# Layer 0 of a two-layer graph network: seven products for eight in its maps, edges counted by pairs of columns, and a residual added by a DMA

## The chip, the cores and the metric

The kernel runs on one core of one Trainium2 chip. The metric is the device time of one execution in microseconds (us), lower is better. The core has five engines that run side by side and meet at semaphores: PE (matrix products), DVE (vector), ACT (scalar functions), POOL (GpSimd) and SP (which only issues DMAs). ACT and POOL issue DMAs too, and all DMAs share 16 DMA engines.

## The reference

The input is x, 4096 rows of 512, and adj, a 4096 × 4096 matrix of 0 and 1 with about 32 ones a row. Two graph layers follow one another.

```
# layer 0
keep   = (adj > 0) and (cumsum of it along the row <= 64)    # the first 64 neighbours
cnt    = number kept in the row
xj     = leaky_relu((keep @ x) / max(cnt, 1) @ W_nb.T + b_nb)
xi     = leaky_relu(x @ W_line.T + b_line)
x1     = layernorm(x + xi + (xj where cnt > 0, else 0))
# layer 1
Wh     = x1 @ W + b_W
e_ij   = leaky_relu_0.2(Wh_i . a1 + b1 + Wh_j . a2 + b2), minus infinity where adj is 0
out    = layernorm(x1 + softmax_j(e) @ Wh)
```

## The kernel before

All rows are in 32 blocks of 128. Instruction order is written out by hand; each engine takes its instructions strictly in that order, and only semaphores hold it. The program has three stages.

**Maps of layer 0** (the loop over i in 0..31). Since keep @ x @ W_nb.T is keep @ (x @ W_nb.T), the kernel maps x first. For each block, POOL loads x in a turned form into one of three buffers (`load_turned_x`, tile c), DVE finishes the transposition (`turn_x`, tile xt), and PE computes two products, `linear(xt, "nb")` and `linear(xt, "line")` (L345). Each is four f32 matmuls with 512 columns over the four quarters of the contraction; the trace has two records for each f32 matmul. The first product y is kept on the chip as two terms, y_hi (rounded, ACT, L413) and y_lo (the rest, DVE, L435), so that the sums can use a fast format. The second gets its bias on DVE (`line`, L375), leaky_relu on ACT (`bend`, L379), x added on DVE (`own`, L383; x comes in a second, plain load to tile xb), and is written to memory (own_d).

Beside the maps, the adjacency is turned into codes, in 64 steps (32 blocks by two halves of 2048 columns). A step loads 1 MB of int32 (SP, L160), makes 0/1 edges in bf16 (ACT, `edge`, L167), scans along the row a counter that falls by one at each edge and stops at a floor of 2 (DVE, `scan`, L179), multiplies edges by the counter (L184), packs the result to a byte (ACT, `pack`, L202) and stores it (POOL, code_d). A byte of 2 or more means a kept edge, 1 an edge that is beyond the 64th, 0 none. AHEAD = 20 of these steps are placed in the maps. `fold_w` (L361) folds W with a1 and a2, once, in block 0; its result goes to memory (wa_d).

**Sums of layer 0** (the loop over s, 32 rows of blocks × 4 groups). For row block i, a DMA with transposition brings the codes of its 128 rows (ktb, issued on SP two rows ahead, L460), ACT turns 8 blocks of it at a time into 0/1 weights (`make_kt`, L254), and PE adds 64 matmuls for the row (y_hi and y_lo by turns, L521). The remaining code steps are spread over these rows at RATE / 4 a group (`codes_step`; ACT's share of a step waits in a queue and is taken out one part at a time by `codes_late`). A row is finished one row later in five parts on DVE (`finish`): scaled by 1/cnt with bias (L479), leaky_relu (ACT, L472), added to own, which SP has loaded from own_d (L516 and L485), normalized with a power on POOL (rs, L126), written as x1 (POOL, L492), and multiplied with the folded weights (L497).

**Layer 1** follows and is not touched (L825 and L739 are its products).

Of the kernel before, what the change touches and what calls it, by code (L numbers as in the profile page):

```python
# [9 lines left out]
F32 = mybir.dt.float32  # L10
# [10 lines left out]
P = 128  # L21
# [11 lines left out]
def two_layer_adj_gnn(  # L33
# [43 lines left out]
    two, steep, far, neg_half = few[:, 0:1], few[:, 1:3], few[:, 3:4], few[:, 4:5]  # L77
    for k, value in enumerate((2.0, -0.5 * STEEP, -1.5 * STEEP, FAR, -0.5)):
        nc.vector.memset(few[:, k : k + 1], value)
# [57 lines left out]
    with ExitStack() as l0:  # L137
        adj_p = l0.enter_context(tc.tile_pool(name="l0_adj", bufs=2))
        big = l0.enter_context(tc.tile_pool(name="l0_big", bufs=1))
        y_hi = big.tile([P, NB, C], F32R, name="y_hi")  # L140
        y_lo = big.tile([P, NB, C], F32R, name="y_lo")
# [20 lines left out]

        def edge(s):
            if s < NB * NCH:
                b, h = divmod(s, NCH)
                edge_of[s] = adj_p.tile([P, CH], BF16, name="edge")
                nc.scalar.activation(  # L167
                    edge_of[s], loaded.pop(s), AF.Sigmoid, bias=steep[:, 0:1], scale=STEEP,
                    accum_out=cnts[:, h, b : b + 1],
                )  # L170

        def scan(s):
            if s < NB * NCH:
                b, h = divmod(s, NCH)

                left = adj_p.tile([P, CH], BF16, name="left")
                e = edge_of.pop(s)
                end = ends[:, b : b + 1]
                nc.vector.tensor_tensor_scan(  # L179
                    left, two.to_broadcast([P, CH]), e,  # L180
                    NEIGHBORS + 2.0 if h == 0 else end, ALU.max, ALU.subtract,
                )
                nc.vector.tensor_copy(end, left[:, CH - 1 : CH])
                nc.vector.tensor_tensor(left, e, left, ALU.mult)  # L184
                seen_of[s] = left
# [3 lines left out]
        def count(b):  # L189
            two_b = slice(b, b + 2)  # L190
            cnt = stat.tile([P, 2], F32, name="cnt")
            nc.vector.tensor_scalar(cnt, ends[:, two_b], 2.0, -1.0, ALU.max, ALU.mult)
            nc.vector.tensor_scalar_add(cnt, cnt, NEIGHBORS + 2.0)
# [4 lines left out]
        def pack(s):  # L198
            if 0 <= s < NB * NCH:
                b, h = divmod(s, NCH)  # L200
                code = adj_p.tile([P, CH // 2], BF16, name="code")
                nc.scalar.copy(code.bitcast(U8), seen_of.pop(s))  # L202
# [57 lines left out]
        with ExitStack() as la:  # L260
# [3 lines left out]
            AHEAD = 20  # L264
# [15 lines left out]
            def load_own_x(i, queue):  # L280
                xbs[i] = work.tile([P, C], F32, name="xb", bufs=3)
                queue.dma_start(xbs[i], x_blk(i))

            def turn_by_pe(dst, src):

                t = work.tile([P, C], F32, name="t")
# [6 lines left out]
            def turn_x(i):  # L293
                if i < NB:
                    xts[i] = work.tile([P, NC, P], F32, name="xt", bufs=3)
# [46 lines left out]
            def linear(lhs_t, name):  # L342
                pl = ps_acc.tile([P, C], F32, name="acc")
# [13 lines left out]
            def fold_w():  # L357
                for c in range(NC + 1):
                    wn = raw["w"][c] if c < NC else early_rows[2]
                    for k in range(2):  # L360
                        nc.vector.scalar_tensor_tensor(  # L361
                            early_rows[3], wn, 1.0, early_rows[k], ALU.mult, ALU.mult,
                            accum_out=wa[:, k, c : c + 1] if c < NC else ca[:, k : k + 1],
                        )
# [8 lines left out]
            def line(i):  # L373
                lines[i] = work.tile([P, C], F32, name="t")
# [6 lines left out]
            def own(i):  # L381
                y = xbs.pop(i)
                nc.vector.tensor_tensor(y, y, lines.pop(i), ALU.add)  # L383
                nc.gpsimd.dma_start(own_d[i], y)

# [9 lines left out]
            spin(12)  # L395
            turn_x(0)
            turn_w("nb", 2)
            for i in range(NB):
                if i > 1:
                    load_own_x(i - 1, nc.gpsimd)  # L400
                if i > 0:
                    load_turned_x(i + 4)
                    turn_x(i + 2)
                xt = xts.pop(i)
                pys[i] = linear(xt, "nb")
                if i == 0:
                    turn_w("line")
                pls[i] = linear(xt, "line")
# [540 lines left out]
```

## Time and profile before

| What | Value |
|---|---|
| Median of 3 runs | 1600.48 us (1599.47 to 1602.02) |
| Profiled execution | 1600.12 us, of which the span from first to last instruction is 1598.4 us |
| Maps, from the first product to the first sum | 9.6 to about 235 us |
| Sums | about 236 to 700 us |
| Layer 1 | 700 us to the end |
| Busy of the span: PE, DVE, ACT, POOL | 99%, 82%, 58%, 16% |
| Granted PE clock | 0.997 of full |

A line of a group of instructions gives the kernel's line, engine, operation, written and read tile, shape and number, then the busy time, the mean of one in ns, and idle time before it with what ended that. The chain of waits follows the end of the program back through what released each instruction; a piece gives its start, its length and its work. In a timeline a row gives start, length, engine, line, operation and the number merged, and in brackets how long the engine had been idle and what released it.

### The profile page before, as it was taken

To read this page: it belongs to the slowest core of one execution; us is meant where nothing else is said; L and a number is where in the kernel's file an instruction comes from. 1 tells how busy PE (TensorE), PEld (TensorE's weight loads), DVE (VectorE), ACT (ScalarE), POOL (GpSimd) and SP (SyncE) were. 2 spreads that over 40 slices of the span, in tenths; PEclk is the share of its full clock that TensorE was granted. 3 is DMA by queue.
4 is the path that set the end of the run, shared out by engine and by line. 5 is a ranking of instruction groups with operands and counts; after the bars stand their busy time and mean duration, and the time that the engine had idled before them with its cause. 6 is when DMAs were issued, how large, how long until landed. Compare 5 with 4: busy or idle time off the path is not lost.

```text
span 1598.4 us, 18483 instructions
## 1 busy us (share of the span) xinstructions
PE 1579.6 (99%) x6456; PEld 1218.4 (76%) x6456; DVE 1305.4 (82%) x2154; ACT 924.2 (58%) x1086; POOL 260.0 (16%) x396
## 2 busy tenths in 40 slices
PE   8999999999999999999999999999999999999997
PEld 4444448888888888864378888888888888888886
DVE  4999986999999999555888887878888888788863
ACT  2655556777777777514237755557755557655520
POOL 4455531122223122210000000000000000000000
PEclk9999999999999999999999999999999999999999
DMA  8887867676757666444201111111111111211100
GB/s 195 287 259 236 265 217 224 215 220 211 229 189 228 206 215 191 116 103 122 76 27 28 53 54 41 52 36 34 53 47 47 48 28 44 54 41 53 40 7 33
DMA packets 168364, 192.73 MB, mean 121 GB/s; under 512 B 101408, under 2 KB 134464, under 8 KB 160080
## 3 DMA queue, kind: packets, MB, share of 16 engines
q1 hardware_dynamic: 147968, 131.38, 29.4%
q0 software_dynamic: 19728, 59.27, 11.0%
q8 instruction: 50, 0.82, 0.2%
q10 hardware_dynamic: 576, 0.92, 0.2%
q14 instruction: 42, 0.34, 0.1%
HBM read 132.65 MB, written 42.08 MB: 109 GB/s over the span
## 4 chain that ended last, share of the span: by engine, by line
PE 92%; DVE 3%; DMA 2%; issue 1%; ACT 1%; SPq 0%; POOL 0%; DVEq 0%; POOLq 0%; ACTq 0%
PE acc L739 34%; PE acc L521 29%; PE pt L739 14%; PE acc L345 9%; PE acc L825 5%; DMA c<-in_x_dram 1%; DVE left L179 1%; DMA a<-in_L_gnn_W_line_dram 1%; DMA edge<-in_L_gnn_a_dram 0%; DVE edge L361 0%; DVE xt L299 0%; DMA w<-x_d 0%; DVE y_lo L435 0%; DVE t L375 0%; ACT w L635 0%
## 5 line engine op out<-in xcount | busy, mean ns | idle before, releaser
L521 PE MATMUL acc<-y_hi,kt 128*128 128x512 f32 x1016 | 395.2, 389 | 0.0
L521 PE MATMUL acc<-y_lo,kt 128*128 128x512 f32 x1016 | 395.2, 389 | 0.0
L739 PE MATMUL acc<-bt,s 128*128 128x256 f32 x1536 | 342.6, 379 | 0.0
L739 PEld LDWEIGHTS acc<-bt,s 128*128 128x128 f32 x1536 | 291.8, 190 | 39.7
L635 ACT ACTIVATE w<-nat,few 128x1024 f32<-128x1024 uint8 x128 | 136.9, 1135 | 290.1 <-DVE a L699 238.8
L126 POOL TENSOR_TENSOR rs<-ve,few 128x1 f32<-128x1 f32 x64 | 76.2, 1191 | 969.3 <-DVE ve L124 969.2
L739 PE MATMUL acc<-bt,a 128*128 128x256 f32 x1024 | 232.1, 379 | 0.0
L739 PE MATMUL pt<-bt,a 128*128 128x256 f32 x1024 | 231.5, 379 | 0.0
L521 PEld LDWEIGHTS acc<-y_hi,kt 128*128 128x128 f32 x1016 | 190.8, 188 | 39.7
L521 PEld LDWEIGHTS acc<-y_lo,kt 128*128 128x128 f32 x1016 | 190.6, 188 | 39.5
L739 PEld LDWEIGHTS pt<-bt,a 128*128 128x128 f32 x1024 | 194.6, 190 | 26.9 <-issue 0.5
L254 ACT ACTIVATE kt<-ktb,few 128x1024 fp32r<-128x1024 uint8 x124 | 142.9, 1152 | 124.7 <-PE acc L521 107.8
L739 PEld LDWEIGHTS acc<-bt,a 128*128 128x128 f32 x1024 | 194.6, 190 | 26.5
L699 DVE STREAM_TRANSPOSE a<-w 128x1024 f32<-128x1024 f32 x128 | 153.0, 1224 | 57.8 <-ACT w L680 53.2
L627 ACT ACTIVATE w<-w,st_n 128x1024 f32<-128x1024 f32 x128 | 149.4, 1233 | 39.5 <-DVE m L638 39.5
L638 DVE CUSTOM_DVE_ANT_0 w<-e_n,w 128x1024 f32<-128x1024 f32 x128 | 149.6, 1221 | 9.6 <-ACT w L635 8.2
L167 ACT ACTIVATE edge<-a,few 128x2048 bf16<-128x2048 int32 x64 | 127.4, 1991 | 43.4 <-DVE left L184 20.3
L680 ACT ACTIVATE w<-w,nm 128x1024 f32<-128x1024 f32 x128 | 145.4, 1136 | 11.3 <-DVE nm L671 11.3
L179 DVE TENSOR_TENSOR_SCAN left<-few,edge 128x2048 bf16<-128x2048 f32 x32 | 141.3, 4415 | 12.7 <-ACT edge L167 10.9
L179 DVE TENSOR_TENSOR_SCAN left<-few,ends,edge 128x2048 bf16<-128x2048 f32 x32 | 143.2, 4475 | 2.3 <-ACT code L202 2.3
L202 ACT CAST code<-left 128x2048 uint8<-128x2048 bf16 x64 | 120.5, 1882 | 0.0
L345 PE MATMUL acc<-wt_nb,xt 128*128 128x512 f32 x256 | 115.5, 594 | 2.8 <-DVE xt L299 2.0
(135 smaller groups left out, 1521.3 us busy)
## 6 DMA issues: line engine op xcount, KB each, us to landing
a<-in_adj_dram SPq DMA_DIRECT2D x64, 1024.0 KB, 5.3
code_d<-code POOLq DMA_DIRECT2D x64, 256.0 KB, 3.7
nat<-code_d SPq DMA_DIRECT2D x256, 64.0 KB, 2.0
own_d<-xb POOLq DMA_DIRECT2D x32, 256.0 KB, 5.9
w<-x_d SPq DMA_DIRECT2D x128, 64.0 KB, 2.0
c<-in_x_dram POOLq DMA_DIRECT2D x124, 64.0 KB, 5.6
xb<-in_x_dram POOLq DMA_DIRECT2D x31, 256.0 KB, 5.8
own<-own_d SPq DMA_DIRECT2D x31, 256.0 KB, 2.8
```

The source lines that it names most:

```text
L167: nc.scalar.activation(edge_of[s], loaded.pop(s), AF.Sigmoid, bias=steep[:, 0:1], scale=STEEP, accum_out=cnts[:, h, b : b + 1],)
L179: nc.vector.tensor_tensor_scan(left, two.to_broadcast([P, CH]), e, NEIGHBORS + 2.0 if h == 0 else end, ALU.max, ALU.subtract,)
L202: nc.scalar.copy(code.bitcast(U8), seen_of.pop(s))
L254: nc.scalar.activation(kts[s], bytes_.rearrange("p t (i r) -> p t r i", r=2), AF.Sigmoid, bias=steep[:, 1:2], scale=STEEP,)
L345: nc.tensor.matmul(pl, lhs_t[:, k, :], w_t[name][:, k, :], start=(k == 0), stop=(k == NC - 1),)
L521: nc.tensor.matmul(accs[i], kt[:, k // 2, k % 2, :], term[:, j, :], start=(j == 0 and term is y_hi), stop=(j == NB - 1 and term is y_lo),)
L627: nc.scalar.activation(dst, src, AF.Prelu, bias=bias, scale=scale, alpha=0.2)
L635: nc.scalar.activation(w_i, nats[b, i // 2].bitcast(U8)[:, i % 2, :], AF.Relu, bias=far, scale=-FAR)
L638: nc.vector.tensor_tensor_reduce(w_i, e2_n, w_i, 1.0, -3e38, ALU.subtract, ALU.max, m4s[b][:, i : i + 1])
L680: nc.scalar.activation(w_i, w_i, AF.Exp, bias=nms[b][:, i : i + 1], accum_out=z4s[g][:, r, i : i + 1])
L699: nc.vector.transpose(a[:, r].rearrange("p s (i a) -> p i s a", a=SQ), wts[2 * g + r][:, :, ts(k, 8 * SQ)].rearrange("p i (s x) -> p i s x ...
L739: nc.tensor.matmul(banks[g][n], lhs[:, j, :], bt[:, 4 * k + j, rhs, :], start=(k == 0 and j == 0 and n == mate[0]), stop=(k == NP - 1 and ...
```

## The change

**Seven products.** Blocks 2 to 25 are taken in 12 pairs. A pair's x is a 2 × 2 matrix of quarters (two blocks of rows by two halves of the contraction), and the two weights are another (two halves of the contraction by nb and line). Their product takes seven products of quarters where it took eight, by Winograd's form; each is two matmuls. Sums of the weights (t1, t2, t4, and t3 in the place of w12) are made once, sums of x (s1, s2, s4, and a21 in place) for each pair, all on DVE. The products add in PSUM: bank_y, bank_z, bank_w and three banks taken in turn for x_g. Between products, ACT copies a bank to another or to SBUF and puts the line's bias into bank_z, and DVE adds a line's part into bank_w. A pair's last products stand in the next pair's step, where its line's bend, own and y terms are too. Blocks 0 and 1 and the last six keep the old form; the y terms of the last six lie in the room that the sums had.

**Pairs of columns.** `edge` writes even columns to the first half of the tile and odd columns to the second (it reads int32 at a step of two). `scan_sums` adds both halves and scans 1024 sums with a floor of 3; `scan_codes` adds the odd edge back for the even column's counter and multiplies. `pack` writes its bytes at a step of two. The threshold that tells a kept edge moves from 1.5 to 2.5.

**x by a DMA.** `own` no longer adds x (but for block 31), and the second load of x in the maps goes. In the sums SP loads x itself into the own tile, and one group later POOL issues a DMA that reads own_d and adds it to the tile.

**Order.** `fold_w` is cut in parts that stand in pair 1. AHEAD is 14 and RATE 57/32. In each pair from the second on, one code step stands in four places between the products.

```diff
-    for k, value in enumerate((2.0, -0.5 * STEEP, -1.5 * STEEP, FAR, -0.5)):
+    for k, value in enumerate((3.0, -0.5 * STEEP, -2.5 * STEEP, FAR, -0.5)):
...
+        ONE_BY_ONE = 6
+        EDGE = NB - ONE_BY_ONE
...
         def edge(s):
...
-                    edge_of[s], loaded.pop(s), AF.Sigmoid, bias=steep[:, 0:1], scale=STEEP,
+                    edge_of[s], loaded.pop(s).rearrange("p (t q) -> p q t", q=2),
+                    AF.Sigmoid, bias=steep[:, 0:1], scale=STEEP,
...
+        def scan_sums(s):
...
+                nc.vector.tensor_tensor(left[:, 0], e[:, 0], e[:, 1], ALU.add)
                 nc.vector.tensor_tensor_scan(
-                    left, two.to_broadcast([P, CH]), e,
-                    NEIGHBORS + 2.0 if h == 0 else end, ALU.max, ALU.subtract,
+                    left[:, 1], three.to_broadcast([P, CH // 2]), left[:, 0],
+                    NEIGHBORS + 3.0 if h == 0 else end, ALU.max, ALU.subtract,
                 )
...
+        def scan_codes(s):
...
+                nc.vector.tensor_tensor(left[:, 0], left[:, 1], e[:, 1], ALU.add)
                 nc.vector.tensor_tensor(left, e, left, ALU.mult)
...
-                nc.scalar.copy(code.bitcast(U8), seen_of.pop(s))
+                nc.scalar.copy(
+                    code.bitcast(U8).rearrange("p (t q) -> p q t", q=2), seen_of.pop(s)
+                )
...
-            AHEAD = 20
+            AHEAD = 14
...
             def own(i):
-                y = xbs.pop(i)
-                nc.vector.tensor_tensor(y, y, lines.pop(i), ALU.add)
+                y = lines.pop(i)
+                if i == NB - 1:
+                    nc.vector.tensor_tensor(y, y, xbs.pop(i), ALU.add)
                 nc.gpsimd.dma_start(own_d[i], y)
...
+            def turn_pair(g, r):
+                i = 2 * g + r
+                turn_x(i, (top, low)[r](g) if i < EDGE else None)
+                load_turned_x(i + 3)
...
+            def sums_x(g):
+                a11, a21, a22 = top(g)[:, 0:2], low(g)[:, 0:2], low(g)[:, 2:4]
+                tt(s1, a21, a22, ALU.add)
+                tt(a21, a11, a21, ALU.subtract)
+                tt(s2, s1, a11, ALU.subtract)
...
+            def sum4_x(g):
+                tt(s4, top(g)[:, 2:4], s2, ALU.subtract)
...
+            def product(bank, lhs, rhs, start=False):
+                for k in range(2):
+                    nc.tensor.matmul(
+                        bank, lhs[:, k, :], rhs[:, k, :], start=start and k == 0, stop=k == 1,
...
+            tt(t1, w12, w11, ALU.subtract)
+            tt(t2, w22, t1, ALU.subtract)
...
+            tt(t4, w21, t2, ALU.subtract)
+            tt(w12, w22, w12, ALU.subtract)
+            t3 = w12
...
+            def seven(g, last, codes):
...
+                p = g - 1
...
+                if new:
+                    product(x_g, top(g)[:, 0:2], w11, start=True)
+                if old:
+                    y_low = y_terms(2 * p, bank_y)
+                    y_low()
+                if new:
+                    turn_pair(g + 1, 0)
+                    nc.scalar.copy(bank_y, x_g)
+                if old:
+                    product(x_p, low(p)[:, 0:2], t3)
+                codes[0]()
+                if new:
+                    turn_pair(g + 1, 1)
+                    product(bank_z, s1, t1)
+                if old:
+                    tt(tp, tp, x_p, ALU.add)
+                if new:
+                    nc.scalar.copy(tg, bank_z)
+                    nc.scalar.copy(bank_z, bias_line)
+                if old:
+                    nc.scalar.activation(tp, tp, AF.Prelu, alpha=SLOPE)
+                    product(bank_w, s4, w22)
+                codes[1]()
+                if old:
+                    nc.scalar.activation(t0, bank_w, AF.Prelu, alpha=SLOPE)
+                    own_pair(2 * p + 1, tp)
+                if new:
+                    sum4_x(g)
+                    product(x_g, s2, t2)
+                codes[2]()
+                if old:
+                    own_pair(2 * p, t0)
+                if new:
+                    tt(bank_w, tg, x_g, ALU.add)
+                if old:
+                    product(x_p, low(p)[:, 2:4], t4)
+                if new and 2 * g + 2 < EDGE:
+                    sums_x(g + 1)
+                codes[3]()
+                if old:
+                    y_terms(2 * p + 1, x_p)()
+                if new:
+                    product(bank_y, top(g)[:, 2:4], w21)
...
+            for g in range(1, EDGE // 2):
...
+                if g == 1:
+                    steps = [
+                        lambda: (load_adj(1), fold_w(0)),
+                        lambda: (fold_w(1), fold_w(2)),
+                        idle[0],
+                        lambda: (fold_w(3), fold_w(NC), fold_end(), edge(0)),
+                    ]
+                elif g > 1:
+                    steps = [
+                        lambda: (load_adj(q + 2), edge(q + 1)),
+                        lambda: scan_sums(q),
+                        lambda: pack(q - 1),
+                        lambda: scan_codes(q),
+                    ]
+                    done[0] += 1
+                seven(g, False, steps)
...
+                codes_until(AHEAD if i >= EDGE + 2 else AHEAD - 2 + i - EDGE)
...
-        RATE = 25 / 16
+        RATE = 57 / 32
...
-                    nc.sync.dma_start(owns[i], own_d[i])
+                    nc.sync.dma_start(owns[i], x_blk(i))
+            if g == 3 and i < NB - 1:
+                nc.gpsimd.dma_start(owns[i], own_d[i], accum_op=ALU.add)
```

## The prediction

> **What bounds the kernel now.** I read the page's busy line first, then the chain of waits in order of time, then a table of windows, then the timelines of the early maps, because the change rewrites that stage.
>
> ```profile
> PE 1579.6 (99%) x6456; PEld 1218.4 (76%) x6456; DVE 1305.4 (82%) x2154; ACT 924.2 (58%) x1086; POOL 260.0 (16%) x396
> ...
> 84.44 151.33 PE acc L345 x352
> 235.78 464.03 PE acc L521 x2047
> ...
> 100.00:140.00 40.00, 40.00 (x95) 17.76 (x94) 39.52 (x44) 21.54 (x24) 21.95 (x40) 1.00 0.77 252
> 300.00:400.00 100.00, 100.00 (x443) 82.79 (x442) 93.42 (x116) 75.89 (x68) 22.38 (x25) 1.00 0.70 213
> ```
>
> PE is the bound, and the chain confirms what a busy share alone would not: from 84 us to 236 it is nothing but the maps' products (L345), then 464 us of sums (L521). The windows (after the length: PE, PEld, DVE, ACT, POOL busy, clock, DMA share, GB/s) add the runner-up: VectorE is at 99% beside the maps and at 93% beside the sums. Every us of PE that goes is worth a us only while DVE has less to do than PE.
>
> ```profile
> 43.83 3.60 PE L345 MATMUL acc<-wt_line,xt 128*128 128x512 f32 x8
> 48.37 3.70 PE L345 MATMUL acc<-wt_nb,xt 128*128 128x512 f32 x8 [0.94 <-DVE xt L299]
> 51.91 3.60 PE L345 MATMUL acc<-wt_line,xt 128*128 128x512 f32 x8
> 56.60 3.70 PE L345 MATMUL acc<-wt_nb,xt 128*128 128x512 f32 x8 [1.10 <-DVE xt L299]
> ...
> 47.01 0.68 DVE L435 TENSOR_TENSOR y_lo<-acc,y_hi 128x512 fp32r<-128x512 f32 x1
> 47.61 0.70 DVE L299 STREAM_TRANSPOSE xt<-c 128x512 f32<-128x512 f32 x1
> 48.24 0.65 DVE L375 TENSOR_TENSOR t<-acc,bias_line 128x512 f32<-128x512 f32 x1
> 48.81 0.67 DVE L383 TENSOR_TENSOR xb<-xb,t 128x512 f32<-128x512 f32 x1
> 49.41 4.47 DVE L179 TENSOR_TENSOR_SCAN left<-few,ends,edge 128x2048 bf16<-128x2048 f32 x1
> ...
> 349.10 4.60 POOL L126 TENSOR_TENSOR rs<-ve,few 128x1 f32<-128x1 f32 x1
> ...
> own<-own_d SPq DMA_DIRECT2D x31, 256.0 KB, 2.8
> x_d<-own POOLq DMA_DIRECT2D x31, 256.0 KB, 2.4
> ```
>
> Start to start, a map (8 records, 4 matmuls) takes 3.43 us, and PE stopped twice, 0.94 and 1.10 us, for a transpose stuck behind a scan. DVE instructions start 0.58 to 0.62 us apart; I use these spacings for its load.
>
> **What the Trainium skill says.** (1) "VectorE: DVE Perf Modes", The perf-mode tier table: a bf16 tensor_tensor of 2048 takes 1224 ns, two elements a cycle, f32 one. The trace agrees: L184 1225 ns, f32 L375 of 512 654 ns. My estimate from that page's count (N/2+151 cycles at 0.96 GHz) for the new 1024-wide bf16 add is 0.69 us. (2) "SBUF — State Buffer", the note on cachelines under the DMA port swizzle: lines are 16 bytes and two hits in each suffice. An int32 step of 8 bytes has two. The trace shows only the kin: kt reads uint8 at a step of two bytes, 1152 ns. (3) Same page, Who interferes with whom: a DVE instruction with two SBUF inputs holds up a GpSimd instruction that reads SBUF. The trace shows it: rs takes 0.56 us, but 4.60 beside the scan above. (4) "Collectives: The Full Stack", The bandwidth ceiling: an add in the DMA needs two source reads. No accumulating DMA is in this trace.
>
> **The change, part by part.**
>
> *Products.* Blocks 0 and 1 and 26 to 31 keep 8 matmuls each; 12 pairs take 7 products of 2 matmuls, 14 for 16. So 24 matmuls, 48 records, go. The chain gives 151.33/352 = 0.430 us a record: **−20.6 us** on the bound. A pair now takes 14 × 0.86 = 12.0 us of PE, formerly 13.8, if the operands are early.
>
> *DVE beside the maps, per pair.* Before: 4 instructions a block, 2 × (0.60 + 0.63 + 0.57 + 0.60) = 4.8 us, and 1.4 code steps of 5.84 (4.45 + 0.15 + 1.23), together 13.1 of 13.8. After: y_lo and transpose twice, 2.5; two 512-wide adds on PSUM, nearest row L375, 1.2 (the one that writes PSUM is new: 0.58 to 0.75 each); four 256-wide adds at 0.425 (L612), 1.7; a code step. That step scans half as many, (4.42 − 0.15)/2 + 0.15 = 2.3, plus 0.15, two new adds at 0.69 and L184's 1.23: 5.05. With counts (0.2) **10.7 of 12.0**. DVE gains room instead of losing it.
>
> *Order on PE.* With the pair starting at 0, I put the queues against each other. ACT copies y_hi at 0.1, DVE's y_lo ends 1.4, two transposes 2.7, the add on tp waits for t3's product and ends 4.2, the scan 7.3, s4 7.7; the add into bank_w waits for s2·t2 (8.6) and ends 9.3; s1, a21, s2 of the next pair 10.5, codes 12.3, y_lo 12.9. PE wants bank_w settled at 13.8, s1 at 15.5, bank_y's copy (2.4) at 6.9, tp's at 8.6. All are 4 us or more early. ACT has y_hi 2 × 0.57, three copies 1.7, two Prelu 1.25, edge 2.2, code 1.9: 8.2 of 12.0. POOL loses one xb issue a block and issues 11 × 0.56 = 6.2. Zero on the path; DVE's 1.3 us spare is the cover. Were it gone, PE would wait for s1 first, but with 4 us in hand.
>
> *Front of the stage.* t1, t2, t4 and t3 are four 1024-wide f32 adds (estimate 1.22 each by page (1)'s count), and fold_w (L361, ten of 0.74) moves from 18.7 us into pair 1. I follow both queues from the trace. PE ends the maps of block 1 at 26.7 as before. DVE then does line(1) to 27.4, t4 and t3 to 29.8, two transposes and the first six folds to 35.5, s4 to 35.9, bank_w to 36.6, s1 to s2 37.8, the last four folds 40.8, y_lo of block 2 41.4. ACT's bias reaches bank_z at 28.7, where PE wants it at 28.4: 0.35 lost. Pair 1 has four products (pair 0 has none to finish), so PE wants bank_w at 35.6: 1.0 lost. ACT can refill bank_y at 42.1, wanted at 41.8: 0.35 lost. Together +1.7. The two waits shown above (2.0) should go, as the x loads start earlier and have no xb between them. The wa_d write moves with the fold: issued at 24.5 us it landed 11.2 us later; now it goes out at 41, in front of edge 2 and x block 9. A wait of 5 us on ACT or DVE there is about what PE has in hand: +1.0, bounds 0 and +5. Sum for the front **+0.7**, from −2 to +5.
>
> *Sums stage.* Its products are the same 2048, 464 us. AHEAD falls from 20 to 14 and RATE rises from 50/32 to 57/32, so codes end in row 28 both times. Per row of 14.5 us: DVE 13.55 (93.4%) + 57/32 × 5.05 − 50/32 × 5.84 = 13.4; ACT 11.0 + 7/32 × 4.06 = 11.9; both below 14.5. rs is held by a scan half as long. The extra 7/32 step (1.25 MB) adds about 0.9 us to the DMAs' 10.2 a row. The first code is due far later than it is made; the margin near row 29 is one to two steps, as before. Zero.
>
> *x by DMA.* In the maps 31 DVE adds and 31 POOL loads go (counted above). In the sums SP loads x where it loaded own_d: zero. The accumulating DMA is new, on POOL, after SP's load: 31 issues. POOL is idle most of the time. Its landing: at best x_d's 2.4 to own's 2.8 us, at worst two reads at the busy maps' 5.9 (own_d's landing there), 11.8. I take 5. In the trace it would go out after rs at 353.7, and L485 wants it at 364.0: 9 to 10 us. Behind it on POOL stand x_d of the row before and codes, and for those SP's next own and ktb. With 5 us all is hidden: 0; engine share +0.7 to +2 us of a row, giving 12 to 13.1 of 14.5.
>
> *The rest.* Constants 3 and −2.5, count, and the restored w12 (1.2 us on DVE under nb of block 26) cost nothing: PE has 3.4 us of product beside the last.
>
> *Sum.* The profiled execution took 1600.12 (span 1598.4 and 1.7 around); −20.6 + 0.7 = 1580.2. The median of the runs is 0.36 higher: **1580.5**.
>
> **The rivals.**
>
> *A. Part is lost again.* The wa_d burst, late x blocks, or DMA bursts in the sums (share 70% before, up to 90% after) outrun PE's 4 us. For it: DMA share 1.02 in 40 to 50 us, landings to 14.4 us. Against: PE lost just 2 us there with DVE at 99%. Two or three waits of 3 to 5 us: 1585 to 1597, say 1590.
>
> *B. The accumulating DMA stops DVE: slower.* L703 waits for it once a row, and behind it stand the scans. The cycle rs → accumulate → own → stats → rs takes 3.6 us and the landing L; it fits 14.5 us up to L = 10.7. Each us beyond costs a us in each of 31 rows, after some 15 us of code margin. It passes the gain of 20 at L = 10.7 + 35/31 = 11.8, just my upper bound. At 13 us: 1580 + 71 − 15 = 1636. Against it: 256 KB transfers land in 2.4 to 2.8 us here.
>
> *C. The pairs of columns are dear.* If stepped int32 reads run at half rate, an edge gains 1.7 us, ACT goes to 14.9 a row, and 0.4 × 29 rows give 1592; if the stepped byte writes do too, 1680. If the bf16 adds ran at one a cycle, DVE would go to 15.3: 1603. Against: pages (1) and (2), and kt.
>
> *D. The products aren't shortened.* If waits at each of 84 products cost 0.2 us, 17 us return: about 1597. The present maps have the same kind of waits and start 3.43 us apart without a gap.
>
> **How the numbers follow.** Full gain, 1577 to 1585: 0.66. A: 0.17. D or a mixture ending near 1600: 0.03. B: 0.08. C: 0.06, two thirds of it slower or level. A measurement can tell some 0.2% (3.2 us) from no change: faster 0.84, same 0.04, slower 0.12. The range takes the full case and A: 1576 to 1597.
>
> **What would show it.** Chain: the maps in one piece to about 216 us where they ended at 236, then the sums, still 464 us without a gap. Rows: 12-us pairs; DVE in the maps below 92%; the scan of 1024 near 2.3 us, adds near 0.69; edge still 2.0, code 1.9. The accumulate should land in 3 to 8 us, and DVE's own should not wait for it. Wrong if PE waits more than 5 us in all for DVE or ACT during the maps, or at all in the sums.

## The result, and the profile after

The changed kernel takes **1581.8 us** (1579.91 to 1582.52) where the kernel before, beside it, took 1601.0: ratio 0.9879, 95% interval 0.9862 to 0.9896. Its profiled execution took 1579.91 us, with a span of 1578.1.

The page's busy line, and then the chain of waits in order of time (start, length, work; the long pieces):

```profile
PE 1558.7 (99%) x6408; PEld 1209.3 (77%) x6408; DVE 1257.6 (80%) x2304; ACT 953.7 (60%) x1123; POOL 240.6 (15%) x397
```

```profile
44.49 130.71 PE acc L489 x300
183.79 34.33 PE acc L371 x80
218.12 464.24 PE acc L741 x2048
682.36 41.21 PE acc L1045 x96
```

PE has 48 records fewer and DVE 48 us less, and the sums are still one piece of 464.2 us. But the maps' piece begins only at 44.49: PE stopped just ahead of it. For all that follows I use two marks in the trace, the first product of the maps (its start varies from 9.3 to 12.0 us between executions, with the loads of the weights) and the first sum. **Maps**, between the two: 225.59 us before (9.62 to 235.21), 207.65 after (9.91 to 217.56), so 17.94 less. **Sums**, from the first sum to layer 1: 465.39 before, 464.80 after.

The table of windows (after the length: PE, PEld, DVE, ACT, POOL busy, granted clock, DMA share, GB/s):

```profile
40.00:60.00 20.00, 17.38 (x37) 7.34 (x36) 13.54 (x23) 13.12 (x19) 7.00 (x13) 0.91 0.74 134
...
80.00:120.00 40.00, 40.00 (x94) 17.67 (x93) 34.16 (x54) 27.58 (x37) 21.57 (x40) 1.00 0.63 204
...
300.00:400.00 100.00, 100.00 (x443) 82.77 (x442) 91.59 (x147) 82.85 (x71) 24.46 (x34) 1.00 0.86 257
```

Beside the steady pairs DVE is at 85% where it was at 99%, and beside the sums at 92%; PE is full in both. The one bad window is the first: PE lacks 2.6 us and its clock is low. PE's timeline there:

```profile
32.58 3.60 PE L489 MATMUL acc<-wt_nb,xt 128*128 128x512 f32 x8
36.45 1.98 PE L489 MATMUL acc<-wt_line,xt 128*128 128x512 f32 x4 [0.28 <-DVE acc L574]
38.27 1.88 PE L489 MATMUL acc<-hi,lo 128*128 128x512 f32 x4
39.99 1.88 PE L489 MATMUL acc<-wt_line,lo 128*128 128x512 f32 x4
44.49 2.54 PE L489 MATMUL acc<-hi,lo 128*128 128x512 f32 x4 [2.62 <-ACT acc L548]
46.82 3.07 PE L489 MATMUL acc<-hi,xt 128*128 128x512 f32 x4
49.73 3.60 PE L489 MATMUL acc<-wt_nb,xt 128*128 128x512 f32 x8
```

Groups of four records start 1.72 us apart as a rule, and 1.82 where the first of them follows a stop. Behind the stop of 2.62 us (for L548, ACT's refill of bank_y) the next two groups take 2.33 and 2.91 from start to start: in this execution the stop is followed by a low clock that costs another 1.7 us. The queue of ACT tells why the refill came late:

```profile
40.37 2.13 ACT L175 ACTIVATE edge<-a,few 128x2048 bf16<-128x2048 int32 x1 [6.80 <-DVE edge L386]
42.41 0.19 ACT L175 ACTIVATION_READ_ACCUMULATOR edge<-a,few 128x1 f32 x1
42.50 0.56 ACT L417 CAST y_hi<-acc 128x512 fp32r<-128x512 f32 x1
43.87 0.57 ACT L548 COPY acc<-acc 128x512 f32<-128x512 f32 x1 [0.81 <-DVE y_lo L418]
```

The first edge step stands in front of y_hi on ACT and waits for DVE's fold (L386; the fold's tiles are the edge tiles), though the product that y_hi reads (the first half of PE's row at 32.58; the other half is the next pair's first product) had ended at about 34.5. y_lo waits for y_hi, the refill for y_lo, PE for the refill.

The groups (busy us, mean ns, then idle before and its cause) and the DMA rows (KB, median us to landing) of the new operations:

```profile
L175 ACT ACTIVATE edge<-a,few 128x2048 bf16<-128x2048 int32 x64 | 136.2, 2129 | 11.8 <-DVE edge L386 6.8 <-issue 2.7 <-DVE left L206 1.5
...
L194 DVE TENSOR_TENSOR_SCAN left<-few,ends,left 128x1024 bf16<-128x1024 f32 x32 | 75.2, 2351 | 1.1
...
L193 DVE TENSOR_TENSOR left<-edge 128x1024 bf16<-128x1024 bf16 x64 | 43.6, 682 | 9.7 <-ACT code L223 9.7
...
L736 POOL DMA_DIRECT2D own<-own_d x31 | 28.7, 925 | 17.2 <-DMA own<-in_x_dram 16.3 <-issue 0.8
```

```profile
own<-own_d POOLq DMA_DIRECT2D x31, 256.0 KB, 5.1
x_d<-own POOLq DMA_DIRECT2D x31, 256.0 KB, 4.7
```

The scan takes half, the new adds 0.68 us, and the accumulating DMA lands in 5.1 us. The edge step costs 0.14 us more than before (1991 ns), where the prediction had expected it unchanged.

### The profile page after: what moved, and what is told of

The parts are those of the page before. It is cut to its first block, busy times and chain, and to the rows that moved or that the text cites. A ratio compares the mean times of both kernels' runs of the same rounds, so it can differ in the third digit from the quotient of the medians.

```text
span 1578.1 us, 18600 instructions
## 1 busy us (share of the span) xinstructions
PE 1558.7 (99%) x6408; PEld 1209.3 (77%) x6408; DVE 1257.6 (80%) x2304; ACT 953.7 (60%) x1123; POOL 240.6 (15%) x397
## 4 chain that ended last, share of the span: by engine, by line
PE 95%; DMA 2%; DVE 2%; ACT 1%; issue 1%; SPq 0%; POOL 0%; POOLq 0%; DVEq 0%; ACTq 0%
PE acc L959 35%; PE acc L741 29%; PE pt L959 14%; PE acc L489 8%; PE acc L1045 5%; PE acc L371 2%; DMA a<-in_L_gnn_W_line_dram 1%; DMA c<-in_x_dram 1%; PE pt L371 0%; DMA w<-x_d 0%; DVE edge L386 0%; ACT w L855 0%; DMA own_d<-t 0%; DVE c L809 0%; POOL c L298 0%
## 5 line engine op out<-in xcount | busy, mean ns | idle before, releaser
L741 PE MATMUL acc<-y_hi,kt 128*128 128x512 f32 x824 | 320.5, 389 | 0.0
L741 PE MATMUL acc<-y_lo,kt 128*128 128x512 f32 x824 | 320.5, 389 | 0.0
L126 POOL TENSOR_TENSOR rs<-ve,few 128x1 f32<-128x1 f32 x64 | 46.7, 730 | 945.8 <-DVE ve L124 933.1
L741 PEld LDWEIGHTS acc<-y_hi,kt 128*128 128x128 f32 x824 | 154.7, 188 | 32.2
L741 PEld LDWEIGHTS acc<-y_lo,kt 128*128 128x128 f32 x824 | 154.6, 188 | 32.1
L175 ACT ACTIVATE edge<-a,few 128x2048 bf16<-128x2048 int32 x64 | 136.2, 2129 | 11.8 <-DVE edge L386 6.8
L1045 PE MATMUL acc<-w,c 128*128 128x512 f32 x232 | 100.3, 593 | 2.6 <-DVE c L809 2.6
L1045 PEld LDWEIGHTS acc<-w,c 128*128 128x128 f32 x232 | 43.9, 190 | 58.8 <-issue 52.1
L206 DVE TENSOR_TENSOR left<-edge,left 128x2048 bf16<-128x2048 bf16 x64 | 78.4, 1225 | 2.2
```

Source lines behind the costliest of these rows:

```text
L175: nc.scalar.activation(edge_of[s], loaded.pop(s).rearrange("p (t q) -> p q t", q=2), AF.Sigmoid, bias=steep[:, 0:1], scale=STEEP, accum_ou ...
L741: nc.tensor.matmul(accs[i], kt[:, k // 2, k % 2, :], term[j], start=(j == 0 and term is y_hi), stop=(j == NB - 1 and term is y_lo),)
L1045: nc.tensor.matmul(pws[s], x1t[:, m, :], ws[:, m, :], start=(m == 0), stop=(m == NC - 1))
```

## The experiments

The theory: the 24 matmuls that go are the whole gain; the other two parts bring little by themselves, but make the room on DVE without which the seven products could not be kept fed; what is missing in the maps is one order on ACT. The rivals are in each expectation. Each ratio is to the kernel before on the same chip, whose median was 1601.0 us beside the kernel after and 1601.6 to 1601.7 in the other comparisons. The stages are read from one profiled execution each.

| Kernel | Median us | Ratio to before (95%) | Maps us | Sums us |
|---|---|---|---|---|
| before | 1601.0 | 1 | 225.59 | 465.39 |
| after | 1581.8 | 0.9879 (0.9862–0.9896) | 207.65 | 464.80 |
| x1_eight | 1597.9 | 0.9979 (0.9971–0.9987) | 223.84 | 465.39 |
| s1_seven | 1614.6 | 1.0084 (1.0069–1.0099) | 212.01 | 494.1 |
| x2_columns | 1600.2 | 0.9994 (0.9986–1.0003) | 206.88 | 485.2 |
| x3_dve_add | 1594.6 | 0.9955 (0.9938–0.9972) | 213.97 | 468.4 |
| f1_edge | 1580.2 | 0.9869 (0.9855–0.9884) | 205.74 | 464.81 |
| f3_table | 1576.4 | 0.9842 (0.9829–0.9856) | 202.80 | 464.80 |
| f4_write | 1577.0 | 0.9847 (0.9834–0.9861) | 202.98 | 464.79 |
| a2_twice | 1625.7 | 1.0149 (1.0136–1.0163) | 207.65 | 505.5 |
| a3_thrice | 1772.8 | 1.1058 (1.1021–1.1096) | 207.65 | 649.4 |
| p1_behind | 1580.9 | 0.9868 (0.9852–0.9885) | 206.94 | 464.80 |
| p2_late | 1582.3 | 0.9875 (0.9861–0.9890) | 207.64 | 466.0 |

### The other two parts alone, and the seven products alone

x1_eight is the kernel before with pairs of columns and x by a DMA:

```diff
-                    left, two.to_broadcast([P, CH]), e,
+                    left[:, 1], three.to_broadcast([P, CH // 2]), left[:, 0],
...
-                    nc.sync.dma_start(owns[i], own_d[i])
+                    nc.sync.dma_start(owns[i], x_blk(i))
+            if g == 3 and i < NB - 1:
+                nc.gpsimd.dma_start(owns[i], own_d[i], accum_op=ALU.add)
```

> The kernel before with two parts of the change, pairs of columns and x added by DMA, but with eight products a pair. Theory (only the 24 matmuls that go are worth time): about 1600, -2 to 0 against before, the 2 us being the two stops of the early maps, which may go because DVE has 2 x 0.60 less per pair and a scan half as long. DVE beside the maps falls from 99% to some 85%, the sums stay at 464 us. Rival (the relief of DVE and ACT in the sums is itself worth time): 1590 or less, and fewer us in the sums.

Measured: 1597.9, 3.7 less than before, a little more than expected. Maps 1.75 us shorter (of the two early stops one is gone), sums to the hundredth the same, although DVE fell there from 93% to between 83 and 86%: here room on an engine that is not the bound is worth nothing. The rival is out. The rest of the 3.7 I could not place in one trace.

s1_seven is the other half, the kernel after with both parts undone (in full the diffs of the next two kernels together):

```diff
-                    left[:, 1], three.to_broadcast([P, CH // 2]), left[:, 0],
+                    left, three.to_broadcast([P, CH]), e,
...
-                    nc.sync.dma_start(owns[i], x_blk(i))
-            if g == 3 and i < NB - 1:
-                nc.gpsimd.dma_start(owns[i], own_d[i], accum_op=ALU.add)
+                    nc.sync.dma_start(owns[i], own_d[i])
```

> The kernel after with its two other parts undone together: edges counted column by column, x added on DVE in the maps, no accumulating DMA; so only the seven products are left of the change. Theory (the other parts are what pays for the seven products on DVE): 10.7 + 0.8 + 1.2 = 12.7 us of DVE in a pair of 12.0, 0.7 x 12 = 8 us lost in the steady pairs, 6 to 10 at the front as in the kernel with x on DVE alone, and in the sums the 18 to 20 of the kernel with columns one by one: 1610 to 1620, slower than before. Rival (the losses overlap, since both are waits for DVE): 1600 to 1605, no change against before. Rival (without the accumulating DMA the sums go better): below 1600.

Measured: 1614.6, **slower than before**, with 48 records fewer on PE. PE's waits in the stretch of the sums, then the windows:

```profile
PE acc L732 <- ACT kt L266: 20.2, 11, 4.6
```

```profile
80.00:120.00 40.00, 39.62 (x93) 17.38 (x93) 39.62 (x57) 22.52 (x30) 22.14 (x42) 1.00 0.79 243
...
500.00:600.00 100.00, 93.19 (x399) 75.30 (x398) 94.19 (x115) 72.81 (x66) 21.01 (x23) 0.98 0.69 216
```

That the total came out as expected is luck, for its terms did not: 4.4 us more than after in the maps, where 14 to 18 were expected, and 29 in the sums, where 18 to 20 were. In the maps DVE at 99% was still nearly enough; the debt is paid in the sums, where 11 times the weights kt are not there, since their codes are late. About 8 of the 9 us above the next kernel's loss in the sums lie at their head, where that kernel has no stop: PE stops there for 1.28 and 4.56 us, with a low clock behind the second stop, ahead of which ACT had waited for the codes:

```profile
243.33 2.19 ACT L266 ACTIVATE kt<-ktb,few 128x1024 fp32r<-128x1024 uint8 x2 [12.52 <-DMA ktb<-code_d]
```

These codes may be late because of the last blocks of the maps, where DVE waited 13.0 us in four times for x in its plain form; that was not tried. Nor was another order for the kernels with a part undone, which keep AHEAD at 14 and RATE at 57/32, though DVE at 99% in the steady pairs of s1_seven leaves no room for more code steps there.

So x1_eight gains 3.7, s1_seven loses 13, and both together gain 19.2: the parts are no sum, one pays for the other.

### One part undone at a time

x2_columns, the kernel after with edges column by column:

```diff
-                nc.vector.tensor_tensor(left[:, 0], e[:, 0], e[:, 1], ALU.add)
...
-                    left[:, 1], three.to_broadcast([P, CH // 2]), left[:, 0],
+                    left, three.to_broadcast([P, CH]), e,
...
-                nc.vector.tensor_tensor(left[:, 0], left[:, 1], e[:, 1], ALU.add)
```

> The kernel after with edges counted column by column, as before the change (scan of 2048, no pair adds, plain edge and code). Theory (pairs of columns are what lets DVE follow the shorter rows of work): in the maps a pair asks DVE for 10.7 + 0.8 = 11.5 of 12.0 us and PE still loses nothing, or little; in the sums DVE's load is 13.55 + 57/32 x 5.84 - 50/32 x 5.84 = 14.8 to 14.9 us a row of 14.5, so 0.3 to 0.4 us a row over 28 rows: +8 to +12, about 1592. Rival (the codes have enough margin, DVE's load is over-counted): +0 to +2, about 1582. A second rival: in the maps a scan of 4.4 us cannot be passed, PE waits for s1 and a21 behind it in each pair, some 1 us x 12: +12 in the maps, none in the sums.

Measured: 1600.2, all of the loss in the sums (+20.4). The maps are 0.8 shorter, but only because this execution lacks the 1.7 us of low clock behind the stop at the front; without that difference they would be about 0.9 longer, far from the 12 of the second rival, which is out. The theory has the right place and half the size. DVE's wait for rs in the sums of this kernel and, in the second line, of the kernel after, and a window of this kernel:

```profile
DVE own L131 <- POOL rs L126: 14.0, 19, 0.8
DVE own L131 <- POOL rs L126: 14.7, 19, 1.3
```

```profile
500.00:600.00 100.00, 94.88 (x407) 76.93 (x406) 94.82 (x116) 72.65 (x66) 30.43 (x29) 0.98 0.85 234
```

DVE is full at 95%, not at 100: in 19 rows it stands some 0.7 us for rs, as it does in the kernel after, a wait that I had left out. 14.85 and 0.7 is 15.5 of 14.5 us, by this estimate 1 us too much in such a row instead of 0.35; and the clock falls to 0.98 in the window, in which PE stops. The chain of waits agrees. In the kernel after it is PE's products throughout the sums; here, from 296 to 624 us, its long pieces are DVE's scans, and where DVE stands for rs, rs is in it too:

```profile
329.53 4.34 DVE left L186
...
337.26 0.57 POOL rs L126
...
338.40 4.40 DVE left L186
```

x3_dve_add, the kernel after with x added on DVE:

```diff
-                if i == NB - 1:
-                    nc.vector.tensor_tensor(y, y, xbs.pop(i), ALU.add)
+                nc.vector.tensor_tensor(y, y, xbs.pop(i), ALU.add)
...
+                if old:
+                    load_own_x(2 * p + 1, nc.gpsimd)
+                    load_own_x(2 * p, nc.gpsimd, room_lo[:, 5])
...
-                    nc.sync.dma_start(owns[i], x_blk(i))
-            if g == 3 and i < NB - 1:
-                nc.gpsimd.dma_start(owns[i], own_d[i], accum_op=ALU.add)
+                    nc.sync.dma_start(owns[i], own_d[i])
```

> The kernel after with x added to the line map on DVE in the maps again (a 0.60 us add a block, x loaded by POOL), and no accumulating DMA in the sums. Theory (the accumulate is hidden, DVE's room in the maps is not needed in full): DVE goes from 10.7 to 11.9 of the 12.0 us of a pair, PE loses 0 to 5 us in the maps; in the sums nothing is gained. 1582 to 1587. Rival (the accumulating DMA costs the sums something): below 1580, with a shorter span of the sums. Rival (at 99% DVE cannot keep up with waits in both directions): about 1 us a pair, 12 us, 1594.

Measured: 1594.6, so the theory fell. It is the size of the last rival, but not by its mechanism: in the steady pairs (80 to 120 us) DVE is at 39.34 of 40 us and PE loses nothing. The profiled execution, 1591.5, is the fastest of the four, and what the others lost beyond it no trace shows. Most of the 6.3 us of the maps go at one place, 3.75 for a stop and 1.7 for low clock behind it, seen in PE's and DVE's timelines:

```profile
71.36 3.65 PE L488 MATMUL acc<-wt_line,lo 128*128 128x512 f32 x4 [3.75 <-DVE acc L577]
74.81 1.95 PE L488 MATMUL acc<-hi,lo 128*128 128x512 f32 x4
```

```profile
69.07 0.69 DVE L411 TENSOR_TENSOR lo<-lo,xb 128x512 f32<-128x512 f32 x1 [3.92 <-DMA xb<-in_x_dram]
```

DVE waits 3.92 us for x in its plain form, which POOL had issued 8.6 us before (the median landing of these loads is 3.9), and the add into bank_w stands behind it. The 3.6 us of the sums are a stop of 3.22 for kt at their head. So in the maps what x by a DMA takes away is not 0.6 us of DVE so much as a load with a due time in a stretch where this one landed late. Behind that first stop the sums are no better without the accumulating DMA: the first rival is out.

### What was missing at the front

f1_edge moves the first edge step behind y_hi and the refill:

```diff
-                        lambda: (fold_w(3), fold_w(NC), fold_end(), edge(0)),
+                        lambda: (fold_w(3), fold_w(NC), fold_end()),
...
-                        lambda: (load_adj(q + 2), edge(q + 1)),
+                        lambda: (edge(0) if q == 0 else None, load_adj(q + 2), edge(q + 1)),
```

> The kernel after with one edge step (edge of step 0) moved from the end of pair 1 to the start of pair 2, behind y_hi and the refill of bank_y on ACT. Theory (in the kernel after, PE stands 2.62 us at the refill of bank_y for pair 2, because y_hi of block 2 stands on ACT behind that edge step, which waits for DVE to end the fold; the stretch of low clock that follows, two groups of four records at 2.54 and 3.07 us for 1.88, comes from the stop): the stop falls to 0.3 to 0.6 us and the low clock goes: -2.1 to -4.1, about 1578 to 1580. Rival (the low clock is there anyway): -2.1 alone. Rival (the first step of codes then comes late for its scan and DVE stands later, stopping PE at s1): 0.

Measured: maps 1.91 us shorter, 1580.2, which by itself can't be told from the 1581.8 of the kernel after. The stop of 2.62 and the low clock behind it are gone, but a new stop of 1.43 us stands a little later, as PE's timeline and ACT's show:

```profile
52.38 1.98 PE L489 MATMUL acc<-wt_line,lo 128*128 128x512 f32 x4 [1.43 <-DVE acc L574]
54.20 1.88 PE L489 MATMUL acc<-hi,lo 128*128 128x512 f32 x4
```

```profile
43.20 0.57 ACT L548 COPY acc<-acc 128x512 f32<-128x512 f32 x1 [6.15 <-DVE y_lo L418]
43.79 1.28 ACT L175 ACT_TABLE_LOAD   x1
45.08 2.13 ACT L175 ACTIVATE edge<-a,few 128x2048 bf16<-128x2048 int32 x1
```

PE waits for DVE's add into bank_w (L574), and that for ACT, which does the load and two edge steps first. In the kernel after, ACT loaded the Sigmoid table at 32.28, while its queue stood; here the load has moved into the path with the edge step. I had moved one instruction and not seen that it brings another with it. Behind this stop of 1.43 the next group takes 1.82 from start to start: the clock stays up.

That the low clock went with the stop of 2.62 does not prove that such a stop always brings it. p1_behind, a kernel of the last group of experiments, has the same front. Its PE stands as long and loses nothing behind it:

```profile
46.11 1.98 PE L489 MATMUL acc<-hi,lo 128*128 128x512 f32 x4 [2.61 <-ACT acc L548]
47.93 1.88 PE L489 MATMUL acc<-hi,xt 128*128 128x512 f32 x4
```

Its maps take 206.94 us; beside them the moved edge step is worth 1.2 us and not 1.91.

f3_table has two more moves, the head of the fold to DVE's idle time ahead of line(1), and the table load to pair 1:

```diff
+            fold_w(0)
             line(1)
...
             nc.scalar.copy(bank_z, bias_line)
+            nc.scalar.activation(ca[:, 0:1], few[:, 0:1], AF.Sigmoid)
```

> The kernel of the moved edge step with two more moves: the first part of the fold stands before line(1), where DVE is idle, and a Sigmoid on one column early in pair 1 loads ACT's table (1.28 us in the trace of the moved edge step, where it stood between the refill of bank_y and the two edge steps). Measured from the first product of the maps to the first sum, the kernel after takes 207.65 us and the one with the moved edge step 205.74, with stops of 0.21, 0.29, 1.43 and 0.46 us. Theory (the stop of 1.43 at the add into tp is the table load and the late fold, 1.28 + 1.5 earlier now): it goes, and the 0.29 too; 204.0 to 204.5 in the stage, about 1578 in all. Rival (the stop belongs to the two edge steps in a row, 4.3 us of ACT in front of the copy of tg, whatever is loaded): 205.5.

Measured: maps 202.80, better than expected, **1576.4** in all, and the only wait left in the pairs is the 0.21 us at bank_z. (The stop had been at the add into bank_w, L574, and not at the one into tp, as the expectation has it.) PE's timeline where the stop was:

```profile
43.50 1.88 PE L489 MATMUL acc<-hi,lo 128*128 128x512 f32 x4
45.22 1.88 PE L489 MATMUL acc<-hi,xt 128*128 128x512 f32 x4
46.94 3.60 PE L489 MATMUL acc<-wt_nb,xt 128*128 128x512 f32 x8
50.37 1.88 PE L489 MATMUL acc<-wt_line,lo 128*128 128x512 f32 x4
```

Its interval lies clear of that of the kernel after, if only just (up to 0.9856 against from 0.9862): this version beats both. The rival, that two edge steps in a row are the stop, is out. How much each of the two moves gave is not known, as they were made together.

f4_write also moves the wa_d write to pair 10:

```diff
+            def write_wa():
                 nc.sync.dma_start(wa_d.rearrange("k (c p) -> p k c", p=P), wa)
...
+                                 write_wa() if q == 8 else None),
```

> As the one before, and the write of wa_d (in which each row of memory is 4 bytes) goes out in pair 10 in place of pair 1. Theory (that write holds the DMA engines for some 12 us, so that the load of the matrix for edge 2 comes 2.8 us late and stops PE for 0.46 in pair 3; in pair 10 the same delay meets DVE and ACT with 1 to 2 us spare a pair): the stop in pair 3 goes, -0.5; a wait for a load shows on ACT or DVE near pair 10, and PE loses 0 to 1 us there. Rival (a wait of 3 to 5 us in a steady pair is more than the cover): a stop of 1 us or more near pair 10. For the time of the whole: no difference that the runs can tell.

Measured: maps 202.98 against 202.80, 1577.0 against 1576.4: no difference. The stop in pair 3 was gone in f3_table already, with the write where it was, so I had blamed the write wrongly.

### How late the accumulating DMA may be

```diff
-                nc.gpsimd.dma_start(owns[i], own_d[i], accum_op=ALU.add)
+                for _ in range(2):
+                    nc.gpsimd.dma_start(owns[i], own_d[i], accum_op=ALU.add)
```

> The kernel after, where the accumulating DMA runs twice one after the other (own_d is added twice, so the output has it twice). One landing took 5.1 us in the kernel after, and the prediction lets 10.7 us fit. Theory: about 10.2 us and 0.9 more to issue: near the edge, DVE begins to wait for the accumulate in the rows where the row before was late, 0 to +5 us. Rival (the limit lies lower, since behind the DVE wait stand two code steps, or the landings lengthen each other): +20 us and more. Rival (DVE finds other work, the limit is a whole row of 14.5): 0.

> The kernel after, where the accumulating DMA runs three times one after the other (own_d is added three times, so the output has it three times). Theory (the cycle from rs to the accumulate to DVE's own to the next rs is 3.6 us and the landing, and cannot pass 14.5): landing 15.3 and two more issues of 0.9, about 4.6 to 6.5 us too much in each of 31 rows, less some 15 us of code margin: +127 to +185, near 1710 to 1770, with DVE's own waiting for own_d in each row. Rival (the cycle can stretch over two rows, as own has more than one buffer): 0 to +20.

Measured: the sums take 40.7 us more with two and 184.6 more with three. For two the theory fell; for three it has the size, but by another loop. POOL's timeline with two:

```profile
314.36 0.92 POOL L737 DMA_DIRECT2D own<-own_d  x1 [1.11 <-DMA own<-in_x_dram]
320.71 0.88 POOL L737 DMA_DIRECT2D own<-own_d  x1 [5.44 <-DMA own<-own_d]
321.29 0.88 POOL L710 DMA_DIRECT2D x_d<-own  x1
```

```profile
SPq L734 <- DMA x_d<-own: 217.5, 22, 14.7
```

The second line is from SP's waits (250 to 600 us): it loads the next own only when x_d has landed, as the tile has one twin. POOL stands 5.44 us for the first accumulate, and x_d of the row before is behind it. So there is a loop that the prediction did not draw: own load (issued at 311.06) 3.3, accumulate 6.35, second issue 0.6, x_d 4.56, next own load (325.85): 14.8 us where a row has 14.5, and some rows took 16 to 17. A third accumulate adds about 6 more; 184.6/31 is 5.95. The loop is put together from the rows that I followed; no run gives own another twin to test it. Nor is all of the loss a stop in the sums. With two accumulates 18.9 us are stops for kt, 11 in number, and 13.8 are one stop at the first product of layer 1, which needs the last rows of x1:

```profile
722.47 13.25 PE L1046 MATMUL acc<-w 128*128 128x512 f32 x24 [13.76 <-DVE w L810]
```

But these two runs test POOL's order and not a late landing alone. p1_behind and p2_late do that without moving a byte more: the accumulate is issued one step later, and two (`g == 1` in p2_late):

```diff
-            if g == 3 and i < NB - 1:
-                nc.gpsimd.dma_start(owns[i], own_d[i], accum_op=ALU.add)
+            if g == 0 and i > 0:
+                nc.gpsimd.dma_start(owns[i - 1], own_d[i - 1], accum_op=ALU.add)
```

> The kernel after, with the accumulating DMA of a row issued one step later, behind x_d of the row before in POOL's order; nothing is added to what the DMAs move. In the trace of the kernel after x_d goes out 0.6 to 4.8 us behind the accumulate, and DVE's own comes 10 to 14 us behind it. Theory (the limit of 10.7 us from rs to the landing holds): 5.1 and 0.6 to 4.8 is 5.7 to 9.9, still inside, 0. Rival (what the two runs with more accumulates showed was a lower limit on the landing, and not POOL's order): DVE waits for own in most rows, +20 and more.

> The kernel after, with the accumulating DMA of a row issued two steps later, behind a code write too. In the trace of the kernel after that write goes out 5 to 14 us behind the accumulate, so the landing comes 10 to 19 us behind rs. Theory (limit 10.7 on the landing): DVE's own waits for the accumulate in most rows, by 0 to 8 us, and about half of it, less the margin of the codes of 15 us, reaches PE: +20 to +110. Rival (own of a row can come a row later, as its tile has a twin and PE needs only codes): 0 to +5.

Measured: nothing in either. DVE's waits in the sums of p2_late:

```profile
DVE own L703 <- DMA own<-own_d: 9.1, 5, 3.0
```

In the rows that I followed (302 to 342 us) the accumulate goes out 4.5 to 7.2 us later than in the kernel after, 7 to 10 us behind rs; with the median landing of 5.0 it is there 12 to 15 us behind rs. In all 31 rows DVE waits five times for it, 9.1 us, and PE stops once for 0.7. The rival is right: a row that is late is caught up, because PE needs codes and not own.

## Why the prediction was right, and where not

The time (1580.5 said, 1581.8 measured) and its cause are right. The sum for the profiled execution, 1580.2, met 1579.91 in part because two misses cancel: the front was 2 us worse, and outside the maps 2.3 us went that nobody had promised. Those are for the most part a gap of 0.58 us between the sums and layer 1, and 1.7 us of low clock in layer 1. The chain shows it in the length of 96 records, before (first line) and after:

```profile
772.39 43.16 PE acc L825 x96
753.87 41.47 PE acc L1045 x96
```

The kernels f1_edge and f3_table have the 43.16 again, so this one is chance of the execution.

- **Products, −20.6.** Right. f3_table has no stop to speak of in the pairs and its maps are 22.8 us shorter than before; 2.0 of these are the two stops of before.
- **DVE beside the maps, 10.7 of 12.0.** Right: in a steady pair DVE is idle for 1.7 us, mostly waiting for PE, so it works 10.3. (The same count gave 13.1 for before, where 99% of 13.8 is 13.7, so it is good to some half a us.) The bf16 add that I estimated at 0.69 from the Trainium skill, "VectorE: DVE Perf Modes", The perf-mode tier table, took 0.682; the scan took 2.35 and 2.29 for 2.3. That this room is what keeps the pairs fed is not shown: with DVE at 99% s1_seven lost only 4.4 us in the maps. Where the relief of DVE decides is the sums, as s1_seven and x2_columns show.
- **Order on PE, zero.** Right in the steady pairs: PE waits for nothing in them.
- **Front, +0.7.** This is the term that was mis-sized; it was about +2.7 (20.6 less 17.94). bank_z lost 0.22 for 0.35 and bank_w 0.28 for 1.0, but bank_y 2.62 for 0.35, and 1.7 of low clock came on top, which the prediction had at nothing. The step that failed is "ACT can refill bank_y at 42.1": I had followed DVE's queue to y_lo and not ACT's queue to y_hi, on which the edge step stood and waited for the fold. f1_edge and f3_table show this. The low clock was bad luck in part: p1_behind, with the same stop, was spared it, and its front is about +2.0. The two old stops went, as said. Of the allowance of +1.0 for late loads nothing was used here: DVE waited 3.7 us for x at 58 us, and PE had work enough. In p1_behind, where PE is not held back by the low clock, a wait of 3.5 us at the same place stops PE for 0.73.
- **Sums, zero.** Right: DVE 92% is 13.3 us a row (13.4 said), ACT 83% is 12.0 (11.9 said), DMA share 0.86 from 300 us (0.83 to 0.90 said) but 0.96 from 500, all without a wait of PE. rs fell from 4.60 to 2.62 us beside a scan, which agrees with the skill's "SBUF — State Buffer", Who interferes with whom: it is held while the scan runs, and the scan is half as long.

```profile
302.34 2.62 POOL L126 TENSOR_TENSOR rs<-ve,few 128x1 f32<-128x1 f32 x1
```

- **Accumulating DMA, 5 us, hidden.** Right, 5.1, and DVE's own did not wait for it. Two source reads, as the skill's "Collectives: The Full Stack", The bandwidth ceiling, puts it, would fit 5.1 against the 2.8 us of the plain load before; no run shows that they are the reason. The limit of 10.7 us in rival B was wrong: a landing 12 to 15 us behind rs cost nothing that can be measured, while a POOL that has to wait for the landing costs at once.
- **Rival C** did not come, but a trace of it did: the edge step takes 7% more. x2_columns, the kernel after with plain edges, shows the edge step without the stride:

```profile
L171 ACT ACTIVATE edge<-a,few 128x2048 bf16<-128x2048 int32 x64 | 127.7, 1995 | 42.5 <-DVE left L197 32.0 <-DVE edge L375 6.8 <-issue 3.7
```

By the skill's "SBUF — State Buffer", the note on cachelines, two hits in a line suffice; the measured 2129 against 1995 ns says nearly, not quite. It lies in ACT's spare time.

## What to carry to other kernels

A faster way on the bound engine shortens the time that all others have: count the runner-up's work against the new, shorter row, and pay for it in the same change, or, as here, a gain of 19 us turns into a loss of 13. When an instruction is moved, follow every queue that it stands in, and what the engine does on its way (here a table load), not only the queue of the engine that was stopped. A DMA may land late and cost nothing as long as the work behind it can catch up; a queue that must stand until the DMA has landed, and then issues what others wait for, costs time at once.

## What the runs showed of the hardware that I had not expected

- PE's clock can fall after a stop, but the length of the stop does not settle it. After the stops of up to 1.43 us at the front it stayed. After 2.23 us in layer 1 both were seen (41.47 and 43.16 us for the same 96 records), and so after 2.6 us at the front (low after 2.62 in the kernel after, full after 2.61 in p1_behind). In x3_dve_add it fell after 3.75 us and not after the 3.22 at the head of the sums. Where it fell after one of these single stops, it cost another 1.7 us: in the kernel after the granted clock was 0.50 from 45.79 to 49.19 us, and half of these 3.4 us is 1.7. What else decides is not shown.
- x_d, a write of 256 KB, landed in 2.4 us before; behind an accumulating DMA on the same queue it took 4.7; with the accumulate issued behind it 3.8 (p1_behind), and with the accumulate a step later still 2.8 (p2_late).
- ACT reading int32 at a step of two took 2129 ns for 2048 elements, against 1995 without the step.
- POOL needed 0.92 us to issue an accumulating DMA of 256 KB, and 0.57 for x_d, a plain one of the same size (in the kernel before).
